# A scan block on one NeuronCore: a new order for the opening, the first pairs and the last six pairs

## The chip, the cores and the metric

The kernel runs on one core of one Trainium2 chip. The metric is device time in microseconds (us) of one execution. The kernel before takes 1816.77 us, the median of three runs (1815.91 to 1816.95).

## What is computed

The input x has 4 images of 128 channels and 96 x 96 points, in float32. Each image is normalised over groups of four channels. Then four sequences are made of it (rows forward and backward, columns forward and backward), and each goes through the same block, cut here to what matters:

```python
t = grouped_1x1(x, in_proj_w, in_proj_b)
u, gate = t[:, :256], t[:, 256:]
u = conv_5_taps_per_channel(silu(u))
s, a, b, c = four_products_of(u)              # 32 rows each; a by a sigmoid, b and c by tanh
h = exp(P) * cumsum(b * s * exp(-P))          # P = cumsum(log(a)): a linear recurrence along the sequence
u = u + ssm_out_w @ (c * h + d * s)
u = grouped_1x1(u * sigmoid(gate), mix_w, mix_b)
y = out_proj_w @ u + out_proj_b
out = x + fuse_w @ concat(y of the four sequences) + fuse_b
```

mix, out_proj and fuse are linear and follow one another, so the kernel multiplies their weights once at its start into one matrix per direction, `w_fin`, and the three biases into `b_fin`.

## The kernel before, in words

**Units and pairs.** A sequence of 9216 points is cut into 6 steps of 1536 points and each step into 4 phases `p` of 384 points. A unit is one direction, one step, one phase. Forward and backward run side by side, so a pair `t` (line 812, `pair`) handles two units; there are 4 images x 2 orders x 6 steps x 4 phases = 192 pairs. Every engine's order is written out by hand in the program (`tc.manual_schedule`, line 1088); no scheduler changes it. An engine executes its instructions in that order, so an instruction that waits holds all behind it on its engine.

**What a pair does.** TensorE: the convolution of the first half of the channels as matmuls (`conv` and `conv_less`, weights `band` and `less`), the in-projection of the step after this one (`in_proj`, line 462, called by `front`), the four products (`proj`, line 643). ScalarE: SiLU of the in-projection out of PSUM (`silu`, line 468), the copy of the convolution into `u` (lines 609 and 611), the first of the five taps of the other half of the channels (line 628), the tanh of the products (lines 667 to 673) and the multiplication of `s` with `d` (`scale_s`, line 683). VectorE: the remaining four taps (line 630), the recurrence (`scan`, line 691), and the gating (line 577). GpSimd: the decay, `b*s`, `c*h + d*s` (`outputs`, line 706) and the additions into the accumulator `acc` (line 754).

**The back part lags.** Six pairs (LAG) behind, the back part of pair `t-6` is done: two gate products (`gate`, line 486) with tanh (line 514), `out_of` (line 494), which adds ssm_out into PSUM banks 0 to 3, the gating, and `accumulate` (line 722) with `w_fin`. Pairs 0 to 5 have no back part, pair 6 is the first with one, and the six back parts still open after pair 191 are done in `tail` (line 898). `under` (line 502) is a ScalarE copy that puts `u` into the PSUM banks before `out_of` adds to them; where it isn't used, VectorE adds `u` afterwards (line 576).

**PSUM.** There are 8 banks. Banks 0 to 3 hold `out_of`; 0 and 1 are also where the taps are summed; 4 and 5 hold the four products in steady state; 6, 7, 2 and 3 take the in-projection.

**The opening** (`load_x`, line 294; `start`, line 993). The image comes in ten DMAs on SyncE's queue, VectorE takes statistics of each 384 columns (line 298), then `stats_finish` (line 180) makes mean and variance into scaled in-projection weights `wn` and biases `bn`. Behind x on the same queue stand the output weights `fuse`, the weights `main`, then the first `x_in` rows. TensorE runs matmuls on x whose result nobody reads (`filler`, line 996) until the statistics are there. In the gaps of the statistics it makes `w_of` (`outer`, line 1002), and between the first SiLUs `w_fin` (`inner`, line 1010). Then come 16 SiLUs, the taps of pair 0 and pair 0's four products; the in-projection of step 1 stands between them (line 653).

**The tail.** For each of the six pairs: `out_of`, gating (VectorE), `under` for the next pair (ScalarE), `accumulate`, the copy of its result (line 735 or 737) and an addition on GpSimd for one direction, on VectorE for the other. `z_copy` (line 909) copies the output of the recurrence from partitions 0 to 63 to partitions 64 to 127.

Of the kernel before, what the change touches and what calls it, by code (L numbers as in the profile page):

```python
# [56 lines left out]
R = 4  # L57
# [10 lines left out]
def conv_preact_kernel(  # L68
# [18 lines left out]
    accf = acc.rearrange("p h r m -> p (h r m)")  # L87
    x_in = [big.tile([P, R, N + 1], F32, name=f"x_in{s}") for s in range(2)]
# [65 lines left out]
    gmask = wp.tile([P, 4], F32, name="gmask")  # L154
    nc.gpsimd.memset(gmask, 1.0)
# [13 lines left out]
    stats, free = {}, [FRONT[1]]  # L169
# [10 lines left out]
    def stats_finish(b):  # L180
# [12 lines left out]
        nc.vector.tensor_copy(mean, pm[:, 0:1])  # L193
        dev = sp.tile([P, 1], F32, tag="dev", name=f"dev_{b}")
        nc.vector.tensor_sub(dev, mv[:, 0:1], mean)
        ex = sp.tile([P, 1], F32, tag="ex", name=f"ex_{b}")
        nc.vector.scalar_tensor_tensor(ex, dev, dev, mv[:, 1:2], ALU.mult, ALU.add)
        gm4 = sp.tile([P, 4], F32, tag="gm4", name=f"gm4_{b}")
        nc.vector.tensor_scalar_mul(gm4, gmask, mean)
# [9 lines left out]
        if b == b0:  # L209
# [4 lines left out]
            nc.vector.reciprocal(inv, std)  # L214
        else:
# [11 lines left out]
        yield  # L227
# [11 lines left out]
        product(pb[:, 0:4], wn, gm4)  # L239
        if b == b0:  # L240
            for g in range(4):
                for q in range(R):
                    mm(pb[:, 4 + g : 5 + g], q, wn[0:32, 32 * g : 32 * g + 32], mean[0:32, :], True, True)
            nc.vector.tensor_sub(bn, b_in, pb[:, 0:8])
        else:
# [10 lines left out]
        nc.vector.tensor_scalar_mul(bn[:, 2:4], bn[:, 2:4], 0.5)  # L256
# [8 lines left out]

    def load_front(step, s, r, q):
        if fresh(step):
            un = units[step * UB + s]
            nc.sync.dma_start(
                x_in[s][r, q, :], xs[un["b"], un["lay"], r, q, bass.ds(un["st"] * N, N + 1)]  # L270
            )
# [22 lines left out]
    def load_x(chunks):  # L294
        for c, n in chunks:
            nc.sync.dma_start(accf[:, bass.ds(c * SC, n * SC)], xr[b0, :, bass.ds(c * SC, n * SC)])  # L296
            for e in range(c, c + n):
                nc.vector.bn_stats(stats_of(b0)[:, e, :], accf[:, bass.ts(e, SC)])  # L298
# [6 lines left out]
    nc.scalar.activation(first_table, first_table, AF.Sqrt)  # L305
    w_small = load(small, "small", nc.scalar)
    load_x([(0, 1), (1, 1), (2, 1), (3, 2), (5, 2), (7, 3), (10, 4), (14, 4), (18, 4), (22, 2)])
    w_out_fuse = load(fuse, "fuse")
    w_main = load(main, "main")
    for s in range(2):  # L310
        load_front(0, s, half(s), slice(0, R))
    for i in range(UB):
        load_gate(i)
# [29 lines left out]
    for s in range(2):  # L343
# [14 lines left out]
    nc.gpsimd.tensor_scalar_mul(  # L358
        w_proj[:, :, 2 * MH : 3 * MH], w_proj[:, :, 2 * MH : 3 * MH], 0.5
    )  # L360
# [3 lines left out]
    gates = [wk.tile([P, 2, 2, N], F32, tag=f"gate{e}", bufs=1, name=f"gate{e}") for e in range(2)]  # L364
# [7 lines left out]
    def chunks_of(t):  # L372

        un = units[2 * t]
        b, k = un["b"] + 1, t % R
        if un["order"] == "V" and b < B and k > 1:
            return [(b, un["st"] * R + 2 * (k - 2) + e) for e in range(2)]
        return []

    def load_chunks(t):  # L380
        for b, c in chunks_of(t):
            chunks[b, c] = wk.tile([P, SC], F32, tag="xs", bufs=4, name=f"xs_{b}_{c}")
# [52 lines left out]
    def after_front(step, g):  # L435
# [7 lines left out]
        if step > 1:  # L443
# [17 lines left out]
    def in_proj(step, g, s, j, bk):  # L461
        wn = stats[units[step * UB]["b"]][0]
        r = slice(64 * s + 32 * j, 64 * s + 32 * j + 32)
        for c in range(4):
            m, q = (c, g) if j else (g, R - 1 - c if s else c)
            mm(bank(bk), c, wn[r, s, 32 * m : 32 * m + 32], x_in[s][r, q, :], True, True)

    def silu(step, g, s, j, bk):
# [3 lines left out]
            bank(bk)[:, : N + 1],  # L472
            AF.Silu,
# [19 lines left out]

    def out_of(bi, s, j):
        z = tbs[bi]
        r = slice(64 * j + 32 * s, 64 * j + 32 * s + 32)
        nc.tensor.matmul(bank(SSM + 2 * s + j)[:, :N], w_so[r, bass.ts(j, P)], z[r, :],  # L497
# [4 lines left out]
    def under(bi, s):  # L502

        seeded.add(bi)
        nc.scalar.copy(psum[:, SSM + 2 * s : SSM + 2 * s + 2, :N], us[bi][:, s])  # L505

    def sigmoids(bi, to):
# [3 lines left out]
        for s in range(2):  # L511

            for j in (0, 1) if s == 0 or to[0] == GATE[True][0] else (1, 0):
# [30 lines left out]
    def gates_and_out(bi, with_front):  # L544

        to = GATE[with_front]
# [19 lines left out]
    def gating(bi, s):  # L566
# [7 lines left out]
        pz = psum[:, SSM + 2 * s : SSM + 2 * s + 2, :N]  # L574
        if bi not in seeded:
# [14 lines left out]
    def conv(i, banks):  # L590
# [3 lines left out]
        for s in range(2):  # L594
# [21 lines left out]
    def taps(i, ks, first=None):  # L616
# [5 lines left out]
        for k in ks:  # L622
# [6 lines left out]
            else:  # L629
                nc.vector.scalar_tensor_tensor(  # L630
                    us[i][:, :, 1, :] if k == K - 1 else part,
# [9 lines left out]

    def proj(i, banks, apart=False):
# [8 lines left out]
        turns = [(e, j) for j in ((1, 0) if i else (0, 1)) for e in range(2)]  # L651
        apart = apart or not i
        for e, j in sorted(turns) if apart and i else turns:
            if i == 0 and (e, j) == (0, 0):
                first = front_parts(R, (5, 4, 2, 3), half=True)
                next(first)
                next(first)
                first_tap(2)
                for _ in first:
                    pass  # L660
            for c, cols in enumerate(((qb, qb, qa, qa), (qs, qs, qc, qc))[e]):
                first, end = (j == 0, j == 1) if apart else (j == 1, j == 0)
                mm(bank(banks[e]), c, w_proj[:, j, cols], us[i][:, c % 2, j, :], first, end)
# [19 lines left out]
    def scale_s(i):  # L683
        s = tbs[i][0:64, :]
        nc.scalar.activation(s, s, AF.Copy, scale=d_sb[0:64, 0:1])
# [20 lines left out]
    def outputs(i, copy=nc.gpsimd.tensor_copy, engine=nc.gpsimd):  # L706
        ta, tb, p = scans[units[i]["step"]], tbs[i], units[i]["p"]
        engine.tensor_mul(ta[0:64, p, :], tb[64:P, :], ta[64:P, p, :])  # L708
        engine.tensor_add(tb[0:64, :], ta[0:64, p, :], tb[0:64, :])  # L709
# [67 lines left out]
    def pair(t):  # L777
# [13 lines left out]
        if back:  # L791
# [13 lines left out]
        if t:  # L805
            new_u(i)
# [371 lines left out]
```

## Time and profile before

| what | us |
|---|---|
| median of three runs | 1816.77 |
| the profiled execution: its own time | 1816.83 |
| the profiled execution: span from first to last instruction | 1815.0 |
| TensorE busy in the span | 1792.2 |
| ScalarE, VectorE, GpSimd busy | 1563.1, 1444.8, 1428.1 |
| first matmul of any kind starts | 11.73 |
| first in-projection matmul starts | 22.60 |
| first SiLU starts | 23.50 |
| pair 0's four products end on TensorE | 37.40 |
| pair 5's four products start, pair 7's start | 64.69, 85.38 |
| last matmul ends | 1810.02 |

The profile gives the time of each instruction on each engine, counted from the start of the span. "L134" is line 134 of the kernel, a helper through which nearly all matmuls go, so TensorE's groups are told apart by their tiles (`psum<-u,main` are the four products, `psum<-u,w_fin` is `accumulate`, `psum<-x_in,wn` the in-projection). A float32 matmul stands as two instructions. In a window view, a row gives for a stretch of time the busy time of each engine and the number of its instructions, then the granted TensorE clock, the share of DMA engines busy and their rate. In a timeline, a row gives the start, the duration, the engine, the line and the operation, and in brackets how long the engine idled before, and what ended it. A TensorE that is busy need not be at its best: an instruction that takes longer is busy longer.

### The profile page before, as it was taken

To read this page: it belongs to the slowest core of one execution; us is meant where nothing else is said; L and a number is where in the kernel's file an instruction comes from. 1 tells how busy PE (TensorE), PEld (TensorE's weight loads), DVE (VectorE), ACT (ScalarE), POOL (GpSimd) and SP (SyncE) were. 2 spreads that over 40 slices of the span, in tenths; PEclk is the share of its full clock that TensorE was granted. 3 is DMA by queue.
4 is the path that set the end of the run, shared out by engine and by line. 5 is a ranking of instruction groups with operands and counts; after the bars stand their busy time and mean duration, and the time that the engine had idled before them with its cause. 6 is when DMAs were issued, how large, how long until landed. Compare 5 with 4: busy or idle time off the path is not lost.

```text
span 1815.0 us, 56931 instructions
## 1 busy us (share of the span) xinstructions
PE 1792.2 (99%) x24074; PEld 644.7 (36%) x24074; DVE 1444.8 (80%) x1462; ACT 1563.1 (86%) x2748; POOL 1428.1 (79%) x1475
## 2 busy tenths in 40 slices
PE   7999999999999999999999999999999999999998
PEld 3333333333333333333333333333333333333333
DVE  6888878787888887877778888787877788778885
ACT  5888888988888888898888888889888888888974
POOL 3587888788778888788877888878777888887785
PEclk9999999999999999999999999999999999999999
DMA  8555463445975465334696456453476643635434
GB/s 254 179 186 174 150 205 100 162 141 161 316 240 175 158 200 169 123 140 139 220 290 228 141 184 206 119 178 113 153 251 217 227 146 128 195 102 178 149 123 157
DMA packets 148047, 321.17 MB, mean 177 GB/s; under 512 B 14160, under 2 KB 115920, under 8 KB 147792
## 3 DMA queue, kind: packets, MB, share of 16 engines
q1 hardware_dynamic: 147648, 317.48, 53.2%
q8 instruction: 190, 3.11, 0.7%
q14 instruction: 65, 0.53, 0.1%
q10 hardware_dynamic: 144, 0.04, 0.0%
HBM read 185.21 MB, written 132.25 MB: 175 GB/s over the span
## 4 chain that ended last, share of the span: by engine, by line
PE 95%; DVE 2%; ACT 1%; DMA 1%; issue 0%; SPq 0%; DVEq 0%
PE psum L134 82%; PE psum L497 8%; PE psum L491 5%; DVE psum L630 1%; DMA xs<-in_xr 1%; DMA acc<-in_xr 0%; DVE u L577 0%; DVE bn L298 0%; DVE u L630 0%; ACT sil L470 0%; ACT psum L505 0%; ACT psum L628 0%; SPq L296 0%; ACT u L611 0%; PE psum L1004 0%
## 5 line engine op out<-in xcount | busy, mean ns | idle before, releaser
L630 DVE SCALAR_TENSOR_TENSOR psum<-sil,small,psum 128x768 f32<-128x768 f32 x576 | 589.0, 1023 | 28.1 <-ACT psum L628 3.4
L577 DVE SCALAR_TENSOR_TENSOR u<-gate,psum 128x768 f32<-128x768 f32 x376 | 349.8, 953 | 275.1 <-ACT u L609 119.2
L134 PE MATMUL psum<-u,w_fin 128*32 128x384 f32 x6176 | 552.7, 488 | 0.2 <-ACT t L673 0.2
L134 PE MATMUL psum<-u,main 128*32 128x384 f32 x6144 | 534.8, 489 | 0.8 <-DVE u L630 0.8
L754 POOL TENSOR_TENSOR acc<-ys,acc 128x384 f32<-128x384 f32 x374 | 410.8, 1120 | 33.5 <-ACT ys L735 10.8
L708 POOL TENSOR_TENSOR t<-t,t 64x384 f32<-64x384 f32 x191 | 236.4, 1238 | 154.2 <-DVE t L702 70.5
L134 PEld LDWEIGHTS psum<-u,w_fin 128*32 128x32 f32 x6176 | 189.0, 110 | 320.4 <-issue 219.1
L134 PEld LDWEIGHTS psum<-u,main 128*32 128x32 f32 x6144 | 181.9, 109 | 324.0 <-issue 197.2
L505 ACT COPY psum<-u 128x768 f32<-128x768 f32 x352 | 276.7, 799 | 23.3 <-DVE u L630 11.4
L134 PE MATMUL psum<-sil,band 128*32 128x384 f32 x3072 | 285.1, 488 | 0.0
L675 POOL TENSOR_SCALAR t<-tm 64x384 f32<-64x384 f32 x191 | 176.9, 926 | 117.9 <-ACT tm L667 98.7
L709 POOL TENSOR_TENSOR t<-t,t 64x384 f32<-64x384 f32 x191 | 247.0, 1293 | 15.0
L497 PE MATMUL psum<-t,main 32*128 32x384 f32 x1536 | 242.1, 514 | 3.3 <-ACT psum L505 2.6
L628 ACT ACTIVATE psum<-sil,small 128x768 f32<-128x768 f32 x191 | 173.2, 907 | 57.3 <-DVE u L577 49.5
L514 ACT ACTIVATE gate<-psum,bnorm 128x384 f32<-128x384 f32 x384 | 192.1, 582 | 27.0 <-PE psum L491 25.4
L676 POOL TENSOR_TENSOR t<-t,tm 64x384 f32<-64x384 f32 x192 | 195.2, 1016 | 15.3
L630 DVE SCALAR_TENSOR_TENSOR u<-sil,small,psum 128x768 f32<-128x768 f32 x192 | 194.9, 1015 | 7.8
L470 ACT ACTIVATE sil<-psum,bnorm 128x385 f32<-128x385 f32 x384 | 192.1, 584 | 3.5 <-PE psum L134 1.4
L134 PE MATMUL psum<-sil,less 64*32 64x384 f32 x3072 | 168.1, 495 | 0.0
L491 PE MATMUL psum<-x_in,wn 32*128 32x384 f32 x768 | 157.5, 527 | 0.4 <-ACT u L609 0.4
L134 PEld LDWEIGHTS psum<-sil,band 128*32 128x32 f32 x3072 | 90.6, 109 | 169.2 <-issue 95.0
L711 POOL COPY t<-t 64x384 f32<-64x384 f32 x188 | 137.0, 729 | 15.5 <-DVE t L709 3.6
(102 smaller groups left out, 1474.9 us busy)
## 6 DMA issues: line engine op xcount, KB each, us to landing
sil<-sil SPq DMA_DIRECT2D x128, 770.0 KB, 6.5
kept<-gate SPq DMA_DIRECT2D x80, 768.0 KB, 3.7
gate<-kept SPq DMA_DIRECT2D x76, 768.0 KB, 4.8
x_in<-in_xs SPq DMA_DIRECT2D x192, 96.2 KB, 2.5
out<-acc SPq DMA_DIRECT2D x48, 384.0 KB, 8.1
acc<-in_xr SPq DMA_DIRECT2D x39, 384.0 KB, 6.2
xs<-in_xr SPq DMA_DIRECT2D x72, 192.0 KB, 5.5
x_in<-in_xs SPq DMA_DIRECT2D x46, 192.5 KB, 3.4
```

The lines of the kernel that those rows point to most:

```text
L134: nc.tensor.matmul(o[r, : rhs.shape[-1]], lhsT, rhs, start=start, stop=stop, skip_group_check=True)
L470: nc.scalar.activation(sils[step][:, s, j, g, :], bank(bk)[:, : N + 1], AF.Silu, bias=bn[:, 1:2] if j else bn[:, 4 + g : 5 + g],)
L491: nc.tensor.matmul(bank(to)[:, :N], stats[un["b"]][0][r, s, :], x_in[s][r, q, off : off + N], start=True, stop=True)
L497: nc.tensor.matmul(bank(SSM + 2 * s + j)[:, :N], w_so[r, bass.ts(j, P)], z[r, :], start=bi not in seeded, stop=True, skip_group_check=True)
L505: nc.scalar.copy(psum[:, SSM + 2 * s : SSM + 2 * s + 2, :N], us[bi][:, s])
L514: nc.scalar.activation(gv[:, s, j, :], bank(to[2 * s + j])[:, :N], AF.Tanh, bias=bn[:, 2 + j : 3 + j], scale=0.5,)
L577: nc.vector.scalar_tensor_tensor(v, g, 1.0, pz, ALU.add, ALU.mult)
L630: nc.vector.scalar_tensor_tensor(us[i][:, :, 1, :] if k == K - 1 else part, src, w_tap[:, k : k + 1], part, ALU.mult, ALU.add,)
L676: nc.gpsimd.tensor_mul(ta[0:64, p, :], tb[0:64, :], tm[0:64, :])
L708: engine.tensor_mul(ta[0:64, p, :], tb[64:P, :], ta[64:P, p, :])
L709: engine.tensor_add(tb[0:64, :], ta[0:64, p, :], tb[0:64, :])
L754: adder.tensor_add(part, y, part)
```

## The change

*The opening.* `fuse` goes on ScalarE's DMA queue, ahead of everything but `small`. SyncE's queue carries x in nine DMAs (1, 2, 3, 4, 4, 4, 3, 2, 1 chunks of 384 columns), then the in-projection weights, the first in-projection rows in a tile of their own (`x_first`, which later serves as the second `gate` tile), the rest of `main`, and the rows of step 1. `w_of` and `w_fin` are made ahead of the fillers, and four fillers read chunks 10, 14, 18 and 18, so each waits for its chunk; two shorter ones of 256 columns stand between the pieces of the statistics. In the statistics a copy leaves the path, and the bias products take the unscaled weights. One SiLU covers both directions (8 of 128 x 770 in place of 16 of 128 x 385), in the order j=1, then all j=0, then the other j=1. `b_fin` is made after pair 2.

*The head.* `scale_s` moves to GpSimd for the first five pairs. The first tap of pair 1 goes to VectorE. In pair 6 the in-projection gets banks (2, 3, 7, 6), half of its SiLUs stand ahead of the convolution copy and half behind it, and `out_of` stands ahead of the gate products. The statistics of the next image are taken in steps 2 to 5, three chunks a pair, in place of steps 0 to 5, two chunks a pair. The silu tiles of step 0 are written out one at a time.

*The tail.* The banks of `out_of` for the last four pairs rotate over (6,7), (0,1), (2,3). The second half of the last recurrence and its outputs come ahead of the gating, in halves; each `accumulate` is one direction, so that `out_of` of the next pair stands between two of them; the last two units are ended in halves in a mixed order.

```diff
-    load_x([(0, 1), (1, 1), (2, 1), (3, 2), (5, 2), (7, 3), (10, 4), (14, 4), (18, 4), (22, 2)])
-    w_out_fuse = load(fuse, "fuse")
-    w_main = load(main, "main")
-    for s in range(2):
-        load_front(0, s, half(s), slice(0, R))
-    for i in range(UB):
-        load_gate(i)
+    def loads():
+        nc.scalar.dma_start(w_out_fuse, fuse)
+        nc.scalar.activation(first_table, first_table, AF.Sqrt)
+        ask_x((0, 1), (1, 2), (3, 3), (6, 4), (10, 4), (14, 4), (18, 3), (21, 2), (23, 1))
+        nc.sync.dma_start(w_main[:, 0:HID], main[:, 0:HID])
+        for s in range(2):
+            load_front(0, s, half(s), slice(0, R))
+        nc.sync.dma_start(w_main[:, HID:], main[:, HID:])
+        for s in range(2):
+            load_front(1, s, half(s), slice(0, R))
+        for i in range(UB):
+            load_gate(i)
+        for c in range(NSC):
+            nc.vector.bn_stats(stats_of(b0)[:, c, :], accf[:, bass.ts(c, SC)])
...
-        if un["order"] == "V" and b < B and k > 1:
-            return [(b, un["st"] * R + 2 * (k - 2) + e) for e in range(2)]
+        if un["order"] == "V" and b < B and k > 1 and un["st"] > 1:
+            return [(b, 3 * (2 * un["st"] + k - 6) + e) for e in range(3)]
...
+    turning = (6, 0, 2)
+
+    def ssm(bi, s):
+
+        k = bi - NU + 8 + s
+        return turning[k % 3] if bi >= NU - 8 else SSM + 2 * s
...
-        to = GATE[with_front]
+        to = GATE[with_front] if bi else (4, 5, 7, 6)
+        if bi == 0:
+            for s in range(2):
+                for j in range(2):
+                    out_of(bi, s, j)
+            for s in range(2):
+                for j in range(2):
+                    gate(bi, s, j, to[2 * s + j])
+            sigmoids(bi, to)
+            return
...
     def scale_s(i):
         s = tbs[i][0:64, :]
+        if i < 2 * LAG - 2:
+            nc.gpsimd.tensor_scalar_mul(s, s, d_sb[0:64, 0:1])
+            return
...
-        scan(NU // UB - 1, 0)
         scale_s(NU - 2)
+        for part in range(2):
+            scan(NU // UB - 1, part)
+            outputs(2 * first + 4, None, r=bass.ts(part, N // 2))
         ssm_out(first + 1)
+        for held_add in adds:
+            held_add()
         gate_units(first + 1)
-        scan(NU // UB - 1, 1)
-        outputs(2 * first + 4, nc.gpsimd.tensor_copy, nc.vector)
-        outputs(2 * first + 6, None)
+        outputs(2 * first + 6, None, nc.vector)
+        outputs(2 * first + 8, None)
+        product(first, 0, 4)
+        product(first, 1, 5)
+        z_copy(first + 2)
+        product(first + 1, 0, 4)
+        outputs(2 * first + 10, None)
+        add()
         ssm_out(first + 2)
         for n in range(first + 2, end - 1):
             gate_units(n)
+            z_copy(n + 1)
+            product(n - 1, 1, 5)
             add()
-            if n > first + 2:
-                finish(n - 1)
+            product(n, 0, 4)
             ssm_out(n + 1)
...
+        for c in (10, 14, 18, 18):
+            filler(c)
+        next(pieces)
+        next(pieces)
+        filler(18, 256)
+        next(pieces)
+        filler(18, 256)
+        next(pieces)
...
+        order = [(1, 0)] + [(0, g) for g in range(R)] + [(1, g) for g in range(1, R)]
+        spots = (D, A, C, D, A, C, A, C)
```

TensorE's instructions between pair 7 and pair 191 stand in the same order in both kernels, and so do ScalarE's from there on.

## The prediction of this change

> **What bounds the kernel now.** First the page:
>
> ```profile
> span 1815.0 us, 56931 instructions
> PE 1792.2 (99%) x24074; PEld 644.7 (36%) x24074; DVE 1444.8 (80%) x1462; ACT 1563.1 (86%) x2748; POOL 1428.1 (79%) x1475
> PE   7999999999999999999999999999999999999998
> ```
>
> TensorE bounds it, with 22.8 us idle. Second, windows: they tell which stretch is dense.
>
> ```profile
> 200.00:300.00 100.00, 100.00 (x1480) 33.90 (x1476) 80.25 (x81) 87.68 (x161) 82.84 (x83) 1.00 0.56 169
> ...
> 17.50:22.60 5.10, 4.92 (x86) 3.38 (x87) 3.52 (x12) 2.15 (x4) 0.38 (x1) 1.00 1.06 219
> 37.40:67.40 30.00, 29.17 (x480) 10.12 (x472) 26.31 (x28) 27.43 (x54) 10.98 (x11) 1.00 0.82 211
> 67.40:85.40 18.00, 17.02 (x231) 5.89 (x231) 13.53 (x17) 15.22 (x31) 12.55 (x14) 1.00 0.35 117
> ...
> 1785.00:1792.50 7.50, 5.48 (x55) 2.07 (x47) 6.61 (x8) 2.42 (x5) 3.71 (x4) 1.00 0.38 151
> 1792.50:1799.30 6.80, 6.80 (x40) 2.37 (x38) 1.82 (x2) 3.17 (x5) 5.88 (x6) 0.50 0.13 51
> ```
>
> The middle has no idle TensorE, and the order of its instructions doesn't change there. So the change can gain before 85 us and after 1777.6 us, and nowhere else. In the last row TensorE is busy for all 6.8 us but at clock 0.50, on 40 instructions.
>
> Third, the timelines of both ends:
>
> ```profile
> 11.71 6.65 DVE L298 BATCH_NORM_STATS2 bn<-acc 128x6 f32<-128x384 f32 x14 [0.42 <-DMA acc<-in_xr]
> 22.60 4.44 PE L134 MATMUL psum<-x_in,wn 32*32 32x385 f32 x96
> 23.50 0.58 ACT L470 ACTIVATE sil<-psum,bnorm 128x385 f32<-128x385 f32 x1 [0.34 <-PE psum L134]
> 24.29 5.31 ACT L470 ACTIVATE sil<-psum,bnorm 128x385 f32<-128x385 f32 x11 [0.21 <-PE psum L134]
> ```
>
> The last 14 statistics run back to back to 18.37 (call it B): VectorE has fallen behind the arrivals and sets B, not the last arrival, which lands at 16.45 (issue plus time to landing). First SiLU at B+5.13, then one each 0.483.
>
> ```profile
> 1792.05 2.79 PE L497 MATMUL psum<-t,main 32*128 32x384 f32 x8 [2.02 <-ACT psum L505]
> 1794.77 5.02 PE L134 MATMUL psum<-u,w_fin 128*32 128x384 f32 x32
> 1800.58 2.79 PE L134 MATMUL psum<-u,w_fin 128*32 128x384 f32 x32
> ```
>
> The same 32 matmuls take 5.02 after the 2.02 wait and 2.79 six us later.
>
> **What the Trainium skill says.** "TensorE: Matmul & The Clock Gate", Part 1: the array runs at half clock until about one window of 3.4 us was busy, goes back after an idle one, and the windows run free. The trace agrees on the halving (5.02 against 2.79; the first fillers 0.85 an instruction, from 17.6 on 0.43), but the longest idle before the drop at 1792.5 is 2.02, so sparse work is enough. "DMA: Bandwidth & Descriptors", "Queues, rings and completion order": each DMA engine serves its queues in turn, packet by packet. Before, only `small` (42 KB) shares with x, so the trace tests it little. "ScalarE: Activation LUTs", "Rules for kernel authors": about 0.3 us per ACTIVATE and 0.83 ns per element: 0.94 for 770. The trace has 0.907 for 128x768 (L628).
>
> **The tail.** Work first, by starts within dense rows: six sets of `out_of` at 0.85 (L497; 0.93 alone) are 5.1; twelve products of 16 instructions at 1.38 are 16.6; four halves at 0.68 are 2.7. Sum 24.4 from 1777.6: 1802.0 at best. Before ends at 1810.02: 8.0 are lost, of it 3.9 to the half clock (2.79 where 0.93 is usual, 5.02 for 2.79), the rest to waits, 2.02 the longest. The chain there, for each pair, is gating (2 x 0.91), `under` into the same banks (0.80), `out_of`, gating, plus `z_copy` behind GpSimd (2.4 for one `outputs`).
> After, followed by hand in each engine's order, with 0.1 per hand-over: gating of pair 186 ends 1780.5; the two scans 1782.3 and 1784.3 on VectorE, halves of outputs on GpSimd at 1783.7 and 1785.65; `out_of` of 187 waits as now (to 1783.2, 0.5 lost); gating 187 waits behind the second scan, to 1786.1 instead of 1784.6, but what is queued behind it (outputs of 189 on VectorE, to 1787.9) is needed only at 1791. Products of 186 fill TensorE to 1785.95; the third waits 0.85 for its bank (its copy stands behind `under`). `out_of` 188 at 1788.2. From there a round is 0.93 + 2 x 1.38 = 3.7, with ScalarE at 2 x 0.80 + 0.51 + 0.58 = 2.7 and VectorE at 1.82 + 0.56 = 2.4 beside it: `out_of` 189, 190, 191 at 1791.9, 1795.6, 1799.3, last six halves from 1800.2 to 1804.4. With the rotated banks `under` of the first direction no longer waits for the gating before it, and `z_copy` is ready 0.8 to 1.2 ahead. GpSimd's longer queue (two held adds, 2.0) is the cover's limit: its `outputs` of 190 end 1790.0 and of 191 at 1794.4, needed by 1794 and 1798.
> Then the end: before, the four last DMAs land 0.97 to 1.02 apart, the first 2.3 after its issue, the last at 1813.99, 1.0 before the span's end. After, they are issued 0.6 to 1.5 apart, so the last is not queued: 1805.0 + 2.3 + 1.0 = 1808.3. Gain 6.7; I take 0.4 off for waits that I don't see: **6.3** (5.0 to 7.2).
>
> **The opening.** *x:* `fuse` is 524 KB; at the 413 GB/s of x it costs 1.28 if it pushes x back fully. Below 6 us the engines move 256 to 300 GB/s and are idle 0.13 of the time, so up to 0.9 can come back; I take B later by 0.9 (bounds 0 and 1.3): B = 19.3. *Chain:* the copy off the path and a filler of 256 columns (0.75 cold, 0.43 warm) in place of four products (1.09): -0.3. The bias products wait for a small scale, not for `wn`: -0.1. The first SiLU needs both directions; before, the second direction's rows landed at 23.25, and the second SiLU started at 24.29. After, `x_first` has 0.26 MB less ahead and lands at 22.3 by the same rate (0.79 MB in about 4.5), ahead of the matmuls at 22.9. First SiLU: B+4.7 = 24.0. *SiLUs:* 8 at 0.86 (0.907 less overlap) against 15 x 0.483 + pauses; the last ends after 24.0 + 7.9, TensorE's bursts and `conv` parts interleaved (0.5 wait for the last bank). Then `conv_less`, the in-projection of step 1 (1.0) and the four products (2.7) are dense, since taps 0, 4, 1, 2 are summed as SiLUs come and one of 1.02 is left: end at F+11.9 = 35.9. Before: 37.40. `w_fin` (2.05) and 0.96 of `b_fin` have left this stretch; `b_fin` comes back behind pair 2 at 0.4 (24 narrow instructions). GpSimd's multiplication of `w_proj` waits for the rest of `main` (about 23), with edge memsets behind it that are needed from 25 on: no cost. Net gain 1.5 - 0.4 = **1.1** (-0.6 to 2.2).
>
> **The head.** Pairs 1 to 5: their products start 6.26, 5.84, 6.18, 6.04, 5.76 apart, dense work is 5.75. The 6.18 is a wait of 1.65 of VectorE for the chunks of the next image (queued behind 3 MB of silu tiles) and 1.06 of statistics; both move to later steps. ScalarE loses 0.62 a pair; GpSimd takes 0.92 (L675's shape) and has 13.5 of 25 us busy. The first tap of pair 1 on VectorE (1.02) avoids a ScalarE wait. 0.5 + 0.1 + 0.4 + 0.3 = 1.3; pairs 4 and 5 have scans (1.78 + 4.2 a pair on VectorE, over 5.75), so I take **1.1** (0.4 to 1.5). Pair 6: from its in-projection (67.41) to its products (73.85) 6.44, dense 4.7. The gate product waits 0.41 for the bank of the copy L609, behind four SiLUs; after, two SiLUs stand ahead of it, and tanh of banks 4 and 5 then limits: 5.8, gain **0.6** (0 to 1.2). Pair 7 waits 0.57 for the gating of pair 6, which can add `u` 2 us earlier: **0.5**.
> *Statistics later:* 24 pairs get 3 x 0.5 instead of 36 with 2 x 0.5. At steps 2 to 5 VectorE has 4.2 + 1.8 + 1.5 = 7.5 of 9.1 us; no cost. Their DMAs stand on SyncE's queue as before, two pairs ahead.
>
> Sum: 6.3 + 1.1 + 1.1 + 0.6 + 0.5 = 9.6. The profiled execution took 1816.83 (span 1815.0 + 1.8), 0.06 from the median: 1816.8 - 9.6 = **1807.2**.
>
> **Rivals.** *The opening stays cold.* The fillers are fewer, and once warm they end 2 to 3 us before the mean product, which leaves a window about as sparse as the one before 1792.5. Then bursts, copies and `conv` run at half clock for one or two windows of 3.4: 1.5 to 3 lost, 1809.5. Against it: SiLUs hide half of it. *The fuse load costs nothing* (the idle 0.13 and the small packets take it up), B = 18.4: 1 us better, 1806.0. *The tail keeps a wait:* if z copies come late behind GpSimd's adds, one 2 us hole and a half-clocked window of 6.8 us return, half the gain: 1811. *Slower:* three statistics in one pair make VectorE late for the gating in steps 2 to 5. It decides if each of 24 pairs loses more than 9.6 / 24 = 0.4 us; at 0.6 it would be 1822. VectorE's 1.6 us of slack speaks against. That the new order doesn't reach the engines is excluded, the order being written by hand.
>
> **How the numbers follow.** A measurement here tells 0.2% (3.6 us) from no change. Forecast 1807.2 (1805.5 to 1809): 0.50. Cold opening 1809.5: 0.20. Cheap fuse 1806.0: 0.13. Tail wait 1811: 0.11. Slower 1822: 0.06. Below 1813.1 lie all but the last and a part of the tail case: faster 0.89, same 0.06, slower 0.05. For 8 in 10 I leave out the slower case, the far end of the tail case and what lies below 1804.5: 1804.5 to 1811.3.
>
> **What would show it.** Right: TensorE at clock 1.00 from 1780 to the end, `out_of` sets 3.7 apart; statistics ending near 19.3; pair 0's products ending near 36; pair distances 5.8 in the head; same distances after pair 7. Wrong: matmul instructions twice as long between 20 and 32 us; `out_of` waiting for `z_copy`; VectorE waits in steps 2 to 5.

## The result and the profile after

The kernel after takes 1816.74 us, the median of 14 executions (1815.67 to 1818.88), against 1816.75 of the kernel before, also 14. The ratio is 1.0002 [0.9994, 1.0009]: no difference that can be measured. The profiled execution took 1818.43, 1.7 above that median, so sums made from its trace come out 1.6 worse than the medians.

The head of the page, after:

```profile
span 1816.7 us, 56996 instructions
PE 1794.3 (99%) x24108; PEld 644.6 (35%) x24108; DVE 1446.4 (80%) x1452; ACT 1559.7 (86%) x2738; POOL 1441.9 (79%) x1491
```

TensorE is as busy as before, and this hides everything: a matmul at half clock is busy twice as long. The windows of the kernel after (busy time and instructions of each engine, then TensorE's clock, DMA share, GB/s) show it:

```profile
16.90:20.31 3.41, 1.24 (x27) 0.84 (x28) 2.41 (x7) 0.00 (x0) 0.00 (x0) 1.00 1.08 214
20.31:37.37 17.06, 16.22 (x234) 4.73 (x234) 8.55 (x16) 9.38 (x12) 1.34 (x10) 0.50 0.45 95
69.82:88.89 19.07, 19.07 (x267) 7.21 (x261) 13.51 (x15) 17.36 (x35) 17.68 (x17) 1.00 0.33 107
200.00:300.00 100.00, 100.00 (x1473) 34.04 (x1456) 81.10 (x82) 88.17 (x163) 83.58 (x87) 1.00 0.59 172
1791.83:1795.24 3.41, 1.57 (x20) 0.33 (x10) 3.38 (x3) 1.28 (x2) 3.25 (x3) 1.00 0.03 6
1795.24:1798.65 3.41, 3.09 (x20) 1.00 (x24) 2.23 (x4) 1.31 (x2) 3.33 (x4) 0.50 0.00 0
```

There are two stretches at 0.50, not counting the cold start. The first begins at 20.31, behind a window in which TensorE worked 1.24 of 3.41, and lasts 17.06 although TensorE is busy for 16.22 of them. The second is 3.41 long, in the tail, behind a window with 1.57 busy. All 14 executions show a mean granted clock of 0.994 to 0.996 (1.000 would be full clock throughout), so none of them kept it. The middle is as full as before, and from pair 5's products to pair 7's (69.82 to 88.89) no idle time is left.

The statistics and the first SiLUs, from VectorE's and ScalarE's timelines, after:

```profile
9.56 8.49 DVE L331 BATCH_NORM_STATS2 bn<-acc 128x6 f32<-128x384 f32 x18 [0.41 <-DMA acc<-in_xr]
```

```profile
23.58 2.49 ACT L500 ACTIVATE sil<-psum,bnorm 128x770 f32<-128x770 f32 x3 [1.35 <-PE psum L135]
33.15 0.90 ACT L500 ACTIVATE sil<-psum,bnorm 128x770 f32<-128x770 f32 x1 [2.01 <-PE psum L135]
```

VectorE sets the end of the statistics as before, at 18.05. The SiLUs start at 23.58 (before: 23.50), and then wait for TensorE, up to 2.01 at a time.

TensorE's timeline, after, in the opening and head, and then in the tail:

```profile
19.04 0.24 PE L135 MATMUL psum<-mv,gmean 128*32 128x1 f32 x8 [2.24 <-DVE mv L190]
28.60 1.54 PE L135 MATMUL psum<-x_first,wn 32*32 32x385 f32 x16 [0.77 <-ACT sil L500]
37.44 2.79 PE L135 MATMUL psum<-u,main 128*32 128x384 f32 x32
57.01 1.45 PE L135 MATMUL psum<-u,main 128*32 128x384 f32 x13 [1.44 <-DVE u L680]
```

```profile
1791.04 1.50 PE L135 MATMUL psum<-u,w_fin 128*32 128x384 f32 x16 [1.17 <-ACT ys L783]
1795.56 4.29 PE L135 MATMUL psum<-u,w_fin 128*32 128x384 f32 x32 [2.16 <-DVE acc L802]
1800.64 2.79 PE L135 MATMUL psum<-u,w_fin 128*32 128x384 f32 x32
```

A burst of 16 in-projection instructions takes 1.54 at 28.60 (0.88 at full clock, in the run with wide matmuls below), pair 0's products start at 37.44 instead of 34.61, and pair 3 waits for its taps. In the tail 32 instructions take 4.29 behind a wait of 2.16, and 2.79 five us later: the same picture as before, at another place.

Taking the starts of the pairs' products from the traces, the difference to the kernel before falls into five stretches. The last column is an experiment told below, with all remedies at once.

| stretch | forecast | after | all remedies |
|---|---|---|---|
| to the start of pair 0's products | -1.1 | +2.8 | -0.3 |
| pair 0 to pair 5 | -1.1 | +2.3 | -0.1 |
| pair 5 to pair 7 | -1.1 | -1.6 | -1.8 |
| pair 7 to pair 191 | 0 | +0.4 | +0.3 |
| pair 191 to the end of the span | -6.3 | -2.2 | -6.0 |
| sum | -9.6 | +1.7 | -7.9 |

So a part of the gain did arrive, 3.8 us in pairs 5 to 7 and the tail. The opening and pairs 0 to 5 gave back 5.1 in these executions; how much pairs 0 to 5 give back differs from one execution to the next, as the experiment on the silu tiles shows.

### The profile page after: what moved, and what is told of

The parts are those of the page before. It is cut to its first block, busy times and chain, and to the rows that moved or that the text cites. A ratio compares the mean times of both kernels' runs of the same rounds, so it can differ in the third digit from the quotient of the medians.

```text
span 1816.7 us, 56996 instructions
## 1 busy us (share of the span) xinstructions
PE 1794.3 (99%) x24108; PEld 644.6 (35%) x24108; DVE 1446.4 (80%) x1452; ACT 1559.7 (86%) x2738; POOL 1441.9 (79%) x1491
## 4 chain that ended last, share of the span: by engine, by line
PE 95%; DVE 2%; ACT 1%; DMA 1%; issue 0%; SPq 0%; DVEq 0%; ACTq 0%
PE psum L135 82%; PE psum L534 8%; PE psum L521 5%; DVE psum L680 1%; DVE bn L331 0%; DMA sil<-sil 0%; DMA acc<-in_xr 0%; DVE u L627 0%; DVE u L680 0%; ACT u L661 0%; ACT psum L678 0%; ACT psum L542 0%; ACT sil L491 0%; DVE t L756 0%; ACT x_first L551 0%
## 5 line engine op out<-in xcount | busy, mean ns | idle before, releaser
L135 PE MATMUL psum<-u,w_fin 128*32 128x384 f32 (+1 forms) x6192 | 552.6, 486 | 3.5 <-DVE acc L802 2.2
L802 POOL TENSOR_TENSOR acc<-ys,acc 128x384 f32<-128x384 f32 x375 | 411.5, 1117 | 26.6 <-ACT ys L785 7.1
L756 POOL TENSOR_TENSOR t<-t,t 64x384 f32<-64x384 f32 (+1 forms) x192 | 237.2, 1235 | 154.9 <-DVE t L750 71.0
L627 DVE SCALAR_TENSOR_TENSOR u<-x_first,psum 128x768 f32<-128x768 f32 x188 | 174.8, 953 | 140.4 <-ACT x_first L551 66.0
L627 DVE SCALAR_TENSOR_TENSOR u<-gate,psum 128x768 f32<-128x768 f32 x188 | 174.8, 952 | 126.9 <-ACT u L659 67.2
L757 POOL TENSOR_TENSOR t<-t,t 64x384 f32<-64x384 f32 (+1 forms) x192 | 249.4, 1299 | 15.1
L491 ACT ACTIVATE sil<-psum,bnorm 128x385 f32<-128x385 f32 x368 | 183.9, 583 | 4.5 <-DMA sil<-sil 1.8
```

Source lines behind the costliest of these rows:

```text
L135: nc.tensor.matmul(o[r, : rhs.shape[-1]], lhsT, rhs, start=start, stop=stop, skip_group_check=True)
L491: nc.scalar.activation(sils[step][:, s, j, g, :], bank(bk)[:, : N + 1], AF.Silu, bias=bn[:, 1:2] if j else bn[:, 4 + g : 5 + g],)
L627: nc.vector.scalar_tensor_tensor(v, g, 1.0, pz, ALU.add, ALU.mult)
L756: engine.tensor_mul(ta[0:64, p, r], tb[64:P, r], ta[64:P, p, r])
L757: engine.tensor_add(tb[0:64, r], ta[0:64, p, r], tb[0:64, r])
L802: adder.tensor_add(part, y, part)
```

## The experiments

Theory: four causes, independent of one another. (1) In the opening the clock falls, and what follows doesn't bring it back. (2) `b_fin` holds VectorE in front of pair 3's taps. (3) Silu tiles written out one at a time hold a buffer. (4) In the tail VectorE and GpSimd block each other. The chief rivals: the clock counts pauses only, so denser fillers are enough; the clock counts busy time, whatever the matmuls are; and the waits are only signs of something else, so that removing one brings up the next.

### Denser fillers

```diff
-        for c in (10, 14, 18, 18):
+        for c in (10, 14, 18, 18, 18, 18):
             filler(c)
```

> The changed kernel with two more fillers on x ahead of the mean product (six in place of four), nothing else. Theory (the 2.24 us of idle TensorE before the mean product drops the clock to half from 20.3 to 37.4 us): the clock stays at 1.00 through the opening, the bursts take half as long, pair 0's products end at 36 to 37 instead of 40.2, and the whole is 3 to 4.5 us shorter than the changed kernel, 1812.5 to 1814. Rival (the narrow 32x32 in-projection matmuls cannot hold the clock, however dense the fillers are): the clock drops a window or two later, pair 0 ends at 39 or later, under 1.5 us gained, about 1815.5.

Measured: 1817.79, ratio 0.9999 [0.9989, 1.0009]; pair 0's products end at 41.04, 0.8 later than in the kernel after. The wait of 2.24 for the mean product is down to 0.52, and the drop only moves. The windows of this kernel:

```profile
24.62:28.03 3.41, 2.60 (x53) 0.54 (x46) 1.55 (x4) 3.18 (x5) 0.97 (x9) 1.00 0.82 197
28.03:38.27 10.24, 8.81 (x86) 1.39 (x86) 5.25 (x6) 2.62 (x4) 0.00 (x0) 0.50 0.02 5
```

TensorE is busy for 2.60 of 3.41 us, all of it 32x32 in-projection matmuls paced by the SiLUs, and the clock falls all the same. The longest pause inside this window is 0.71. My first theory, that the pause alone was to blame, fell here, and the whole gained nothing. The question is now whether the size of the matmuls counts.

### A hole in the kernel before

```diff
         next(pieces)
-        for n in (512, 512):
-            filler(n)
         next(pieces)
```

> The kernel before with the second group of fillers left out: 4 instructions of 128x512, 1.7 us, between the last statistics and the bias products; nothing else changes, and nothing that they compute is used. Theory: a hole of about 2 us without matmuls in this stretch is what halves the clock, before as after. Then the clock falls to 0.50 at 20 to 21 us, the in-projection bursts take 1.5 in place of 0.77 for 16 instructions, and pair 0's products end at 39.5 to 41 in place of 37.4; whole 1819 to 1820. Rival: the wide matmuls that follow (the products of fuse and the output weights between the pieces of the statistics, 8 x 0.14 each time, and those into w_fin between the SiLUs) hold the clock of the kernel before whatever the fillers do: no drop, pair 0 ends at 37.2 to 37.5, whole as before.

Measured: 1823.90, ratio 1.0036 [1.0024, 1.0048], against 1817.55. The windows of this kernel:

```profile
17.69:21.10 3.41, 1.63 (x33) 1.51 (x34) 2.27 (x7) 0.64 (x2) 0.39 (x1) 1.00 1.06 201
21.10:34.76 13.66, 13.66 (x170) 8.80 (x178) 2.70 (x15) 8.17 (x17) 1.61 (x2) 0.50 0.42 100
```

The mechanism is as expected: two fillers less leave 1.63 busy us in a window (the kernel before has 3.23 there, in 17.56:20.97), and four windows at half clock follow in which TensorE never rests. Pair 0 ends at 43.07 instead of 37.40. So the fillers of the kernel before, 1.7 us of matmuls that nobody reads, were worth 5.7 us in this execution, and the whole became 6.4 slower. Both are larger than expected: pair 0 was to end by 41, and the whole at 1819 to 1820.

### More matmuls, or wider ones

Both have the denser fillers. The first issues each of the last five bursts twice, the second puts one matmul over the whole array ahead of each of these bursts:

```diff
-        def burst(j, g, banks):
-            for s in range(2):
+        def burst(j, g, banks, wide=False, twice=False):
+            if wide:
+                nc.tensor.matmul(bank(banks[0])[:, :256], accf[:, bass.ds(18 * SC, P)],
+                                 accf[:, bass.ds(18 * SC, 256)], start=True, stop=True)
+            for s in (0, 1, 0, 1) if twice else (0, 1):
                 in_proj(0, g, s, j, banks[s])
...
-        burst(*order[3], D)
+        burst(*order[3], D, twice=True)
```

The other four bursts are changed like the last line, and the second kernel has `wide=True` there.

> The kernel after with the fillers of the first experiment, and each of the last five in-projection bursts issued twice (the second time the same values into the same banks), so that TensorE has hardly a pause between 22 and 32 us, but only with narrow 32x32 matmuls. Theory (the clock follows how much of the array works, not whether it works): the clock falls to 0.50 between 27 and 29 us all the same, for 7 to 14 us; bursts of 32 instructions then take 3.0, pair 0 ends at 42 or later. Rival (only pauses count): the clock stays 1.00 up to pair 0; a doubled burst takes 1.53 against 0.86 for its SiLU, so pair 0 ends at 38 to 39.5 with TensorE dense.

> The kernel after with the fillers of the first experiment, and one wide matmul that nobody reads (128 partitions x 128 columns of weights, 256 columns, 2 instructions) ahead of each of the last five in-projection bursts, in the bank that the burst then fills. Theory (width counts): the clock stays 1.00 from 16 us on; a burst with its wide matmul takes 0.77 + 0.43 = 1.2 against 0.86 of its SiLU, so pair 0's products end at 36.0 to 37.7 in place of 40.2 in the profile, and the whole is 2.5 to 4 less than the kernel after if nothing later takes it back; pairs 3 and 5 can take back 1 to 2 of it (the b_fin and silu waits are still there). Rival (only pauses count, or the clock falls for another reason): the drop at 28 stays, pair 0 ends at 41 or later.

Measured: twice 1821.91, ratio 1.0023 [1.0016, 1.0030], pair 0 ends at 45.55. Wide 1814.11, ratio 0.9991 [0.9977, 1.0005], pair 0 ends at 37.06. The windows of the doubled bursts and then of the wide matmuls:

```profile
18.63:22.04 3.41, 2.42 (x73) 1.60 (x79) 1.77 (x9) 1.45 (x2) 0.00 (x0) 1.00 1.07 228
22.04:42.52 20.48, 20.48 (x272) 7.84 (x265) 7.32 (x10) 8.04 (x11) 1.35 (x10) 0.50 0.27 61
```

```profile
19.58:22.99 3.41, 2.90 (x106) 1.78 (x106) 1.22 (x7) 2.02 (x4) 0.39 (x1) 1.00 1.07 230
20.31:37.37 17.06, 16.38 (x284) 5.84 (x286) 9.67 (x16) 12.21 (x18) 1.46 (x11) 1.00 0.52 121
```

The doubled bursts miss in one point: the drop came at 22.04, ahead of them, so this execution doesn't show that doubled bursts fail to hold a clock. One of the 17 executions even took 1816.52 at a mean granted clock of 1.000, so there they held it. What the profiled one shows is about raising the clock: 20.48 us without any pause, first of narrow bursts and then of narrow bursts and convolution, and the clock stays at 0.50 for six windows. (At half clock a dense window holds half the work of a dense one at full clock, so the two can't be set side by side.) With wide matmuls ahead of the bursts the clock stays at 1.00, and pair 0 ends at 37.06 in place of 41.04 with the denser fillers alone.

This pair of runs leaves the second rival open: the wide matmuls also fill pauses, and all windows shown so far would fit a limit of some 2.7 busy us. Other stretches of the same traces rule it out. These two windows kept the clock, and the window behind each ran at 1.00 too. The first is in the tail of the kernel with doubled bursts, the second in pair 3 of the kernel before without two fillers:

```profile
1796.98:1800.39 3.41, 1.80 (x20) 0.44 (x12) 3.38 (x3) 1.28 (x2) 3.25 (x4) 1.00 0.05 19
```

```profile
58.65:62.06 3.41, 1.62 (x21) 0.82 (x25) 3.33 (x5) 1.73 (x3) 0.00 (x0) 1.00 0.55 138
```

A pause of 2.31 us reaches 1.79 into the second window, more idle time than the 0.81 of the window ahead of the drop with denser fillers. Its 1.62 busy us, 21 instructions of the four products on tiles of 128 x 32, were enough; 2.60 us with 53 instructions on tiles of 32 x 32, of nearly as many columns each (385 and 384), were not. So neither the pause nor the busy time nor the number of instructions decides by itself: a matmul of 32 x 32 counts for less than a wider one. It does count, since in the run with denser fillers a window of nearly nothing else (21.20:24.62, 3.01 busy) kept the clock. That the share of the array in use is what is weighed is my reading; by how much, the runs don't tell.

The executions with wide matmuls fall into two groups, ten at 1812.8 to 1815.1 and four at 1820.2 to 1823.7. The mean granted clock is 0.999 to 1.000 in the first and 0.993 to 0.995 in the second, so what sets the second apart is a lost clock; where it is lost, is not on record. What the profiled one shows is the lower group.

### b_fin on ScalarE

```diff
-            nc.vector.tensor_add(b_fin, pf, b_fuse)
+            nc.scalar.activation(b_fin, pf, AF.Identity, bias=b_fuse)
```

> The changed kernel with the addition that makes b_fin after pair 2 on ScalarE instead of VectorE. Theory (on VectorE it waits for a product that stands behind pair 2's products on TensorE, and the taps of pair 3 are queued behind it for 4.2 us): TensorE's wait of 1.4 us ahead of pair 3's products goes, pair distance 2 to 3 falls from 7.97 to about 6.5, 1815.4 in all. Rival (pair 3 waits for its first tap on ScalarE anyway): the wait stays over 1 us, no gain, 1816.7.

Measured: 1816.56, ratio 1.0001 [0.9992, 1.0009]. First VectorE's timeline in the kernel after, then TensorE's with this edit:

```profile
52.61 0.16 DVE L1083 TENSOR_TENSOR b_fin<-psum,small 128x1 f32<-128x1 f32 x1 [4.18 <-PE psum L135]
52.69 3.13 DVE L680 SCALAR_TENSOR_TENSOR psum<-sil,small,psum 128x768 f32<-128x768 f32 x3
```

```profile
55.45 2.79 PE L135 MATMUL psum<-u,main 128*32 128x384 f32 x32
67.21 2.45 PE L135 MATMUL psum<-sil,band 128*32 128x384 f32 x16 [1.98 <-ACT sil L491]
```

After: VectorE stands idle for 4.18 us in front of an addition of 128 x 1, because its product is queued on TensorE behind pair 2's products; the taps of pair 3 are queued behind the addition. With the edit pair 3 starts 6.46 after pair 2 instead of 7.97: the mechanism is right. In the profiled execution the gain is lost again: TensorE then waits 1.98 ahead of pair 5 for a SiLU, which itself waits 3.9 for its tile to be written out, and the pause brings another half-clocked window (67.61 to 71.02). That is the last rival of the list, one wait in place of another. But this execution took 1820.66; it is one of five at 1819.0 to 1820.8, with a clock of 0.993 to 0.994. The other nine stand at 1815.8 to 1816.9 with 0.995 to 0.996, and why these gain nothing, the record doesn't show.

### The silu tiles as before

```diff
-        if step > 0:
+        if step > 1:
             keep_silu(1)
...
         to_keep.extend((0, g) for g in range(R))
+        keep_silu(R)
```

> The changed kernel with the four silu tiles of step 0 written out together at the start, as in the kernel before. Theory (the last of them is written out at 57.8 and landed at 65.4, and step 2's SiLU waits for that buffer 1.76 us): that wait goes, pairs 4 and 5 come 0.5 to 1 us earlier, 1816. Rival (the wait is hidden, and four large transfers at once delay the rows of step 2): no gain or up to 1 us worse, 1816.7 to 1817.7.

Measured: 1817.26, ratio 0.9995 [0.9987, 1.0003]. The SiLU of step 2 in the kernel after:

```profile
65.49 2.00 ACT L491 ACTIVATE sil<-psum,bnorm 128x385 f32<-128x385 f32 x4 [1.76 <-DMA sil<-sil]
```

Step 0's last tile is sent at 57.84 and lands at 65.39; step 2 uses the same buffer. With the edit this wait is gone, and from pair 3's products to pair 5's it takes 12.29 instead of 12.81. That is no gain to rely on: with the tiles still written out one at a time, the same stretch took from 11.69 (denser fillers) to 13.02 (doubled bursts). How long step 2's SiLU waits depends on when it comes, and the whole shows no gain.

### The tail: outputs of pair 189 on GpSimd

```diff
-        outputs(2 * first + 6, None, nc.vector)
+        outputs(2 * first + 6, None)
```

> The changed kernel with one tail step, the outputs of the fourth pair from the end, on GpSimd instead of VectorE. Theory (VectorE and GpSimd, both with two inputs in SBUF, hold each other up: 2.83 and 1.63 us on VectorE in place of 0.90 and 0.88, which delays an addition that a PSUM bank and so TensorE wait for, 2.16 us, and the sparse stretch then halves the clock for 3.4 us): the wait of 2.16 falls under 0.5, the clock stays at 1.00 to the last matmul, from pair 191's products to the end 31.5 to 32.5 instead of 35.1 us, 1813 to 1814 in all. Rival (the same work on GpSimd is late for the copy that the next pair's ssm_out needs): the hole moves to ssm_out, 0 to 1 us gained, 1816.

Measured: 1814.28, ratio 0.9982 [0.9975, 0.9990]. VectorE's and GpSimd's timelines in the kernel after:

```profile
1790.54 2.83 DVE L756 TENSOR_TENSOR t<-t,t 64x384 f32<-64x384 f32 x1
1793.41 1.64 DVE L757 TENSOR_TENSOR t<-t,t 64x384 f32<-64x384 f32 x1
1794.97 0.54 DVE L802 TENSOR_TENSOR acc<-psum,acc 128x384 f32<-128x384 f32 x1
```

```profile
1790.65 1.96 POOL L802 TENSOR_TENSOR acc<-ys,acc 128x384 f32<-128x384 f32 x2
1792.69 1.75 POOL L756 TENSOR_TENSOR t<-t,t 64x384 f32<-64x384 f32 x1
```

Before, the same multiplication and addition took 0.90 and 0.88 on VectorE, and GpSimd was idle beside them; first VectorE's timeline, then GpSimd's, in the kernel before:

```profile
1786.59 0.90 DVE L708 TENSOR_TENSOR t<-t,t 64x384 f32<-64x384 f32 x1
1787.53 0.88 DVE L709 TENSOR_TENSOR t<-t,t 64x384 f32<-64x384 f32 x1
```

```profile
1788.56 0.50 POOL L711 COPY t<-t 64x384 f32<-64x384 f32 x1 [3.62 <-DVE t L709]
```

Now the multiplication takes 2.83, which is 0.90 and nearly the whole 1.96 of GpSimd's two additions: one engine stands while the other works. The Trainium skill, "SBUF — State Buffer", section "Who interferes with whom", says that a VectorE instruction with two SBUF inputs contends with a GpSimd instruction that reads SBUF, and calls the contention for the port pair that they share an exclusive lock. The trace agrees with both. The addition into `acc` (L802) is queued behind the outputs, frees its PSUM bank at 1795.5, and TensorE waits 2.16 for it. With the edit, TensorE's timeline:

```profile
1791.61 2.79 PE L135 MATMUL psum<-u,w_fin 128*32 128x384 f32 x32
1795.18 2.79 PE L135 MATMUL psum<-u,w_fin 128*32 128x384 f32 x32
```

The wait is gone, the clock stays at 1.00, and a round (from one `accumulate` to the next) is 3.57. The span ends 31.3 us behind pair 191's products, in place of 35.1 (after) and 37.3 (before). Of these 3.8 us, 1.6 are the lost clock and not the wait: in the run with wide matmuls the tail still has a wait of 2.12 at the same place, but the window with most of it (1787.69:1791.10) held 1.86 busy us, the clock stayed, and the tail took 33.5. So the same wait costs more or less, depending on where the clock's windows fall. The whole is 0.3 above the 1813 to 1814 that I expected.

### The kernel before with pair 6 and the tail alone

The edit takes from the change only pair 6, the rotated banks and the tail (with the outputs on GpSimd):

```diff
-        nc.tensor.matmul(bank(SSM + 2 * s + j)[:, :N], w_so[r, bass.ts(j, P)], z[r, :],
+        nc.tensor.matmul(bank(ssm(bi, s) + j)[:, :N], w_so[r, bass.ts(j, P)], z[r, :],
...
-        if back:
+        if bi == 0:
+            turned = front_parts(t + R, (2, 3, 7, 6), half=True)
...
+        outputs(2 * first + 6, None)
```

> The kernel before with two parts of the change alone: the order of pair 6, and the tail with the outputs of pair 189 on GpSimd as in the tail experiment; opening, statistics and pairs 0 to 5 as before. If the parts add up: pair 0 ends at 37.4, pair 7 starts 1.6 earlier than before (83.8), the tail is 31.3 in place of 37.3, the whole 1816.8 - 6.0 - 1.6 = 1809.2 (1808.5 to 1810.5). Rival: the time of the tail hangs on where the clock's windows fall, or later pairs take back what pair 6 gained: 1811 or more, with a stretch at clock 0.50 behind 1775.

Measured: 1810.85, ratio 0.9962 [0.9949, 0.9974]. The tail is 31.5 and at full clock, as expected, and pair 5 to 7 takes 1.7 less than before. The whole misses by 1.6: pair 7 starts at 84.78, not at 83.8, because from pair 2's products to pair 4's it takes 1.3 more than before. VectorE's waits between 36 and 70 us in this kernel name a part of it:

```profile
DVE bn L387 <- DMA xs<-in_xr: 2.4, 1, 2.4
```

It was 1.6 in the trace of before. The wait for the next image's chunks, which the change moves away, costs 0.8 more in this execution; the rest stays open.

### All remedies, and then steadier

The four remedies together (wide matmuls with the denser fillers, `b_fin`, silu tiles, outputs); then the same with two fillers of 512 in place of 256 columns and two more wide matmuls; then that with wide matmuls of 128 columns.

> The kernel after with all four remedies at once: the fillers and the wide matmuls ahead of five bursts (their results are used by nobody), b_fin's addition on ScalarE, the silu tiles of step 0 written out as before, and the outputs of pair 189 on GpSimd. If the four causes are the whole of the missing gain, they add up: 1813.0 (the profiled execution with the wide matmuls) - 2.1 (its tail of 33.5 becomes 31.4) - 1.5 (pair 2 to 3: 6.5 in place of 8.0) - 0.5 (pairs 3 to 5) = 1808.9 (1807.5 to 1810), pair 5 starts at 63.5 to 64.3. Rival: behind b_fin another wait takes its place, as when that remedy stood alone (pair 4 to 5 took 9.5): pair 5 starts at 65.5 or later, whole 1810.5 or more. As with the wide matmuls alone, some executions may still lose the clock in the opening: these stand about 10 higher.

> The same with more wide work ahead of the bursts: the two fillers between the pieces of the statistics are 512 columns in place of 256, and a wide matmul stands ahead of the second and third burst too. Theory: the executions with wide matmuls that took 1820 to 1824 had a clock window in 18 to 23 us with too little wide work; then here such executions are rarer or gone (at most 1 in 10 above 1815 in place of 4 in 14), at a cost of 0.2 to 0.6 for the longer fillers: 1808.9 to 1809.5. Rival: they come from elsewhere; as many executions are 8 to 10 above the others as without the wider fillers.

> The kernel with the wider fillers, its seven wide matmuls ahead of bursts cut from 256 to 128 columns. TensorE paced the opening there (a burst with its wide matmul took 1.44, its SiLU 0.86); a wide matmul of 128 columns takes 0.3 less, seven times: 2.1. If half the wide work still holds the clock: no stretch at 0.50 before 1800, pair 0's products end at 37.2 in place of 39.3, all executions near 1809.2. Rival (the amount of wide work in a window decides, and this is too little): a stretch at 0.50 begins between 24 and 32 us in some or all executions, which then take 1815 to 1820.

| kernel | median | executions | pair 0 ends | ratio to before |
|---|---|---|---|---|
| all remedies | 1809.39 | 14 at 1808.88 to 1809.65, 8 at 1816.31 to 1818.62 | 37.10 | 0.9964 [0.9952, 0.9976] |
| wider fillers | 1811.34 | 5 at 1811.21 to 1811.48 | 39.32 | 0.9962 [0.9950, 0.9974] |
| half the width | 1809.90 | 6 at 1809.68 to 1810.05 | 37.80 | 0.9948 [0.9930, 0.9966] |

In the executions that keep the clock the causes add up: 1808.91 in the profiled execution where 1808.9 was expected, pair 5 starts at 64.27 (63.5 to 64.3 expected). With `b_fin` and the silu tiles both mended, pair 2 to 3 takes 6.47 and pair 4 to 5 takes 6.01: the wait that followed the first edit alone in its profiled execution was the one that the second takes away. The 14 lower executions with all remedies show a mean granted clock of 0.999 to 1.000, the 8 upper ones 0.994 to 0.995: what sets them apart is a lost clock. With more wide work none of 5 and 6 executions does (0.999 to 1.000). That fits windows in the opening with too little wide work as the cause, but which windows the upper ones lose isn't on record, so that part isn't shown. The price was 2.2 us, not the 0.2 to 0.6 that I expected: bursts with wide matmuls are 1.44 apart, more than the 0.86 of a SiLU, so TensorE paces the opening. Half the width gives 1.5 of it back (2.1 expected) and still holds the clock. The window of that kernel:

```profile
19.00:37.80 18.80, 18.69 (x310) 7.03 (x314) 9.95 (x20) 12.19 (x17) 1.38 (x10) 1.00 0.91 234
```

It is the lowest of all by its ratio, 8.1 us below the median of the kernel before beside it, though the intervals of the three overlap. They overlap with that of pair 6 and the tail alone too: that the new opening and head, even mended, bring anything beyond those two isn't shown.

## Why the prediction was wrong, point by point

**The tail (6.3 forecast, 2.2 measured).** What failed is the step "outputs of 189 on VectorE, to 1787.9", two operations at 0.9. The duration came from a row in which GpSimd was idle; in the new order GpSimd adds at that time, and the two took 4.5 (1790.54 to 1795.05). "Needed only at 1791" overlooked the addition behind it, which frees a PSUM bank. The rival "the tail keeps a wait" gave 4 us of loss by a 2 us hole and a half-clocked window; the hole came (2.16), but from VectorE, not from the copies of z. The rest of the tail was right: rounds of 3.57 against 3.7. The end was 0.7 too early: I took the last DMA for not queued, but in the trace of the tail experiment the last four land 0.98 to 0.99 apart, the last 3.3 after its issue, not 2.3. And one sum is off without consequence: by the two pairs of numbers given, the half clock cost the tail of before 4.1 (1.86 and 2.23), not 3.9.

**The opening (1.1 gained forecast, 2.8 lost).** The arrivals were right or better: `fuse` cost nothing, the statistics end at 18.05 (19.3 forecast, 18.37 before), as in the case "the fuse load costs nothing". What failed is the term "the last ends after 24.0 + 7.9, TensorE's bursts and `conv` parts interleaved", which takes full clock for granted. I had named the cold opening and given it 0.20, with "one or two windows of 3.4". It lasted five, since I took any busy window to bring the clock back. The window ahead of the drop was visible in my own plan: fillers end 2 to 3 us before the mean product, 1.24 busy us of 3.41, against 1.40 ahead of the drop in the tail of before (1789.08:1792.49), which the rival named as its pattern. That likeness was the better forecast. And even at full clock the new opening gains 0.3 only: what holds the clock takes the time that one SiLU for both directions saves.

**The head (1.1 gained forecast, 2.3 lost).** `b_fin` "comes back behind pair 2 at 0.4" priced its matmuls only. The step also moves a VectorE addition that waits for them, and pair 3's taps are queued behind that: 1.5. This 1.5 is there in every run without the remedy (pair 2 to 3 takes 7.97 or 7.98). The silu tiles "written out one at a time" stood in my description of the change and had no price at all: a SiLU of the kernel after waits 1.76 for its buffer, and once `b_fin` was mended TensorE waited 1.98 in the profiled execution. This part varies: with the same head, pairs 0 to 5 lost from 1.2 (denser fillers) to 2.4 (doubled bursts), and 2.3 in the kernel after. With both mended the head is 0.1 better than before, not 1.1: pair 2 to 3 still takes 0.7 more than the dense 5.75, where the narrow `b_fin` products stand, and the rest is spread over small waits that no run singled out.

**Right.** Pairs 6 and 7: 1.6 gained, 1.1 forecast, and 1.7 with these two parts alone. Statistics of three chunks in steps 2 to 5: no cost; the middle is 0.4 longer in all, 0.35 of it at one place (pair 104), where the slower rival needs 0.4 for each of 24 pairs.

**The clock.** The Trainium skill, "TensorE: Matmul & The Clock Gate", "HAM oscillation — how this bites in real kernels", gives the rule "no PE-idle gaps >~3.4µs". Here stretches at 0.50 are multiples of 3.41 long (3.41, 10.24, 13.66, 17.06, 20.48), which agrees with the page's windows of 3.4. The rule isn't strict enough here: the clock fell behind windows with pauses of 2.0 to 2.2, and with denser fillers behind one whose longest pause was 0.71, while a pause of 2.31 over two windows did no harm elsewhere. The measurement decides.

## What to carry to other kernels

Ahead of a stretch of small tiled matmuls, ask what keeps TensorE's clock up: not only how busy it is, but on which tiles it works in each window of 3.4 us; fillers that look like waste can carry the opening. When a step is moved, write down the engine that each of its instructions waits on, down to an addition of 128 x 1, and what is queued behind it there. And never take the duration of a VectorE operation with two SBUF inputs from a row where GpSimd was idle, if GpSimd will read SBUF beside it.

## What the runs showed of the hardware that I had not expected

- Half clock at a busy TensorE: 20.48 us without pause, with 32x32 matmuls and convolutions of 128x32, at 0.50.
- Ahead of drops TensorE was busy 1.24, 1.40, 1.57, 1.63, 2.42 and 2.60 of 3.41 us. Of the 2.42, 1.4 were the two fillers of 256 columns; the 2.60 were narrow matmuls alone. Windows with 1.62, 1.80 and 1.86 on tiles of 128 x 32 and 32 x 128 kept the clock, and one with 3.01 of nearly only 32 x 32 did.
- The same wait in the tail lost the clock in one kernel (2.16, 1.57 busy in the window) and not in another (2.12, 1.86 busy).
- The executions of one kernel can fall into two groups, 1808.9 to 1809.7 at a mean clock of 0.999 to 1.000 and 1816.3 to 1818.6 at 0.994 to 0.995 with all remedies; with more wide work there was one.
- The second half of the last recurrence on VectorE takes 2.35 beside GpSimd's `outputs`, 1.90 before; GpSimd's addition of 64x192 takes 2.02 there, 0.67 alone.
